# An LSTM step with one half's gates in pairs: half-width blocks, input products 128 steps at a time, and another order of VectorE's queue

## The chip, the cores and the metric

One core of one Trainium2 chip. The metric is the device time of one execution in microseconds; runs are given as the median of several.

## The reference

Two layers over x of shape 2 x 1024 x 256 (N = 2 sequences, T = 1024 steps, D = 256 features), all in float32. The first layer is an LSTM over time, added to its input:

```python
def step(carry, xw_t):
    prev_h, prev_c = carry
    a = xw_t + prev_h @ Wh                 # xw_t = x[:, t] @ Wx + b;  Wx, Wh: 256 x 1024
    i = sigmoid(a[:, :H]);  f = sigmoid(a[:, H:2*H])
    o = sigmoid(a[:, 2*H:3*H]);  g = tanh(a[:, 3*H:])
    next_c = f * prev_c + i * g
    next_h = o * tanh(next_c)
    return (next_h, next_c), next_h
x = x + LSTM(x, h0=cond, Wx, Wh, b)
```

The second layer is a mixture of experts over all 2048 tokens, added to its input: two shared experts (silu(x w1) * (x w3) w2, 512 hidden units each), a router over the token and the condition with sigmoid scores, the two best of eight routed experts (gelu, 256 hidden units each), their outputs weighted by normalised scores, all divided by 4.

## The kernel before

The LSTM is a chain of 1,024 dependent steps and sets the order of everything; the experts' work is put between the steps as filler.

**One step.** The hidden state is kept transposed: 128 partitions, K = 2 halves of features, and the N = 2 columns of one step. As stationary operand a step takes 32 columns (`h_at(t)`), of which only the two of this step are not zero. The recurrent weights stream as moving operand, so that ps[m] (PSUM, one tile for each half m of the units) holds, for each of Q = 4 row groups of 32 rows, the 32 rows of TB = 16 steps x 2 sequences and 4 gates x 32 units as columns. The four matmuls of a block (q = 0..3) go to four row groups. `BLOCKS` gives the order (L541): feature half k, unit half m, columns c0 to c1. k = 0 needs the first h of the step before, k = 1 the second.

After that, for m = 0, 1: VectorE transposes ps[m] in blocks of 32 x 32 (`transpose`, L568), so that units are partitions; ScalarE takes the sigmoid of three gates and the tanh of the fourth for the two rows of this step (`squash`, L571, L572); VectorE multiplies the old cell by the forget gate (`forget`, L575), copies g (`seen`, L579) and makes the new cell by a scan (L580); ScalarE takes its tanh (L588); VectorE multiplies by the output gate and writes h (`output`, L591). All instructions of an engine run in the order in which they are written.

**Input products.** ps[m] of the next 16 steps is begun ahead with bias and x Wx (`project`, L469): in 3 of 16 steps 8 matmuls (bias, then each half of x) take the place of one filler matmul.

**Filler.** In each step up to ROOM = 2 expert matmuls follow the recurrent ones (`fill.run_pe`); where there are none, matmuls on the identity (L556) keep PE busy. Their results are taken up by ScalarE (`fill.act`) and VectorE (`fill.dve`) behind the step's own instructions, by written-down costs: VectorE gets items up to 0.5 us a step. Expert work is queued by groups of 128 steps (64 at the end), each with a number of steps (`PACES`) over which it is spread: `scores` (L236), `shared_up` and `routed_up` (L321), `shared_down` (L377, L383), `routed_down` (L401), `add_expert` (L412); the router's choice is some 28 small VectorE operations (`choose`), queued like the rest or, behind the last step, in `aside`. The last 64 steps' tokens are worked on after the last step.

**Residual.** Every 16 steps POOL adds h to x into x2T (`residual`, L485), which the experts read; `met` (L625) is a VectorE copy of one column that waits for it.

**Loads.** wx on ScalarE's queue; bias, the first 32 steps of x, cond, wh, the rest of x, then all expert weights on SP's queue, at once at the start.

Of the kernel before, what the change touches and what calls it, by code (L numbers as in the profile page):

```python
# [9 lines left out]
F32 = mybir.dt.float32  # L10
# [6 lines left out]
P = 128  # L17
N = 2
# [5 lines left out]
TB = ROWS // N  # L24
E = 8
# [12 lines left out]
ROOM = 2  # L38
WARM = 5
# [5 lines left out]
BLOCKS = [(0, 0, 0, 128), (0, 1, 0, 64), (1, 0, 0, 128), (0, 1, 64, 128), (1, 1, 0, 128)]  # L45


class Fill:
# [19 lines left out]
    def to_dve(self, cost, fn, lag=1):  # L68
        self.add(self.dve, cost, fn, lag)

    def to_aside(self, cost, fn):
        if self.last:
            self.aside.append(fn)
        else:
            self.to_dve(cost, fn)

    def run_aside(self, count):
        for _ in range(min(count, len(self.aside))):
            self.aside.popleft()()
# [21 lines left out]
def lstm_moe_kernel(  # L101
# [23 lines left out]
    xT_sb = const.tile([P, K, T, N], F32, name="xT_sb")  # L125

    b_sb = const.tile([P, 4 * D], F32, name="b_sb")
    one_sb = const.tile([P, ROWS], F32, name="one_sb")
    nc.vector.memset(b_sb, 0.0)
    nc.vector.memset(one_sb, 0.0)  # L130
    nc.vector.memset(one_sb[0:1, :], 1.0)
    xT_v = xT.rearrange("(k p) t n -> p k t n", p=P)
    FIRST = 2 * TB
    nc.sync.dma_start(out=b_sb[0:1, :], in_=b)
    for k in range(K):
        nc.scalar.dma_start(out=wx_sb[:, k, :], in_=wx[k * P : (k + 1) * P, :])
        nc.sync.dma_start(out=xT_sb[:, k, :FIRST, :], in_=xT_v[:, k, :FIRST, :])
# [3 lines left out]
    for q in range(4):  # L141
        for k in range(K):
            cols = slice(max(FIRST, q * T // 4), (q + 1) * T // 4)
            nc.sync.dma_start(out=xT_sb[:, k, cols, :], in_=xT_v[:, k, cols, :])
# [8 lines left out]
    nc.sync.dma_start(out=wr_sb, in_=wrT.rearrange("(k p) e -> p k e", p=P))  # L153
    nc.sync.dma_start(out=rb_sb, in_=rbias.to_broadcast([P, E]))
    nc.sync.dma_start(out=w1_sb, in_=s_w1T.rearrange("(k p) f -> p k f", p=P))
    nc.sync.dma_start(out=w3_sb, in_=s_w3T.rearrange("(k p) f -> p k f", p=P))
    nc.sync.dma_start(out=w2_sb, in_=s_w2T.rearrange("(c p) d -> p c d", p=P))
    nc.sync.dma_start(out=r1_sb, in_=r_w1T.rearrange("(k p) f -> p k f", p=P))
    nc.sync.dma_start(out=r2_sb, in_=r_w2T.rearrange("(c p) d -> p c d", p=P))
# [21 lines left out]
    stepp = ctx.enter_context(tc.tile_pool(name="step", bufs=3))  # L181
    stepsp = ctx.enter_context(tc.tile_pool(name="steps", bufs=2))
# [34 lines left out]
    def experts(t0, S):  # L217
# [42 lines left out]
        def squash():  # L260
            st["s"] = big("s")
            nc.scalar.activation(st["s"], st["z"], AF.Sigmoid)
            for fn in choose():
                fill.to_aside(0.18, fn)
# [131 lines left out]
        def routed_down(i, e2, j):  # L396
            if j == 0:
                st["down"] = bank()
            ps, half, h = st["down"], j // (HR // P), j % (HR // P)
            c = (2 * e2 + half) * (HR // P) + h  # L400
            nc.tensor.matmul(  # L401
                ps[:, half, :], toks(st["h_r"][:, c, :], i), r2_sb[:, c, :],
                start=(h == 0), stop=(h == HR // P - 1), skip_group_check=True,
            )
            if j == 2 * (HR // P) - 1:
                for half in range(2):
                    fill.to_dve(0.5, lambda half=half: add_expert(i, 2 * e2 + half, ps[:, half, :]))

        def add_expert(i, e, ps):
            fill.run_aside(len(fill.aside))  # L410
            acc = st["acc", i]
            nc.vector.scalar_tensor_tensor(  # L412
                acc, ps, st["gate"][:, i, e : e + 1], acc, ALU.mult, ALU.add
            )
            if e % 2:
                fill.let_go()
            if e == E - 1:
                t = t0 + i * (P // N)
                nc.sync.dma_start(out=out_tn[t : t + P // N], in_=acc)
# [27 lines left out]
    SLOT = K * ROWS  # L447
    DIAG = SLOT + N
    hs, diags = [], []
    for i in range(2):  # L450
        flat = const.tile([P, TB * DIAG], F32, name=f"h{i}")
        nc.gpsimd.memset(flat, 0.0)
        hs.append(flat[:, : TB * SLOT].rearrange("p (u k r) -> p u k r", k=K, r=ROWS))
        diags.append(flat.rearrange("p (u s) -> p u s", s=DIAG)[:, :, :SLOT])

    def h_at(t):
        return hs[t // TB % 2][:, t % TB]

    def h_cols(t):
        u = t % TB  # L460
        return h_at(t)[:, :, N * u : N * (u + 1)]
# [3 lines left out]
    def project(ps, grp, k):  # L465
        for m in range(K):
            for q in range(Q):
                cols = slice(q * D + m * P, q * D + (m + 1) * P)
                nc.tensor.matmul(  # L469
                    ps[m][q * ROWS : (q + 1) * ROWS],  # L470
                    one_sb if k < 0 else xT_sb[:, k, grp * TB : (grp + 1) * TB, :],
                    b_sb[:, cols] if k < 0 else wx_sb[:, k, cols],
                    start=(k < 0),
                    stop=False,
                    skip_group_check=True,
                )

    def gates_tile():

        tiles = [gates_ps.tile([P, 4, P], F32, name=f"ps{m}") for m in range(K)]  # L480
        return [a[:, 0] for a in tiles], [a[:, 1] for a in tiles], tiles[0][:, 2:]

    def residual(grp, u0, u1):
        t0 = grp * TB - 1
        nc.gpsimd.tensor_add(  # L485
            x2T[:, :, t0 + u0 : t0 + u1, :],
            xT_sb[:, :, t0 + u0 : t0 + u1, :],
            diags[grp % 2][:, u0:u1].rearrange("p u (k r) -> p k u r", r=ROWS)[:, :, :, :N],
        )
# [23 lines left out]

    nxt_results = results()
# [5 lines left out]
    nxt, nxt_turned, busy = gates_tile()  # L520
# [5 lines left out]
    for k in range(-1, K):  # L526
        project(nxt, 0, k)
    due = 0
    for t in range(T):
        fill.step = t  # L530
        grp, u = divmod(t, TB)
        if u == 0:
            ps, turned = nxt, nxt_turned
            nxt, nxt_turned, busy = gates_tile()
            fresh = True
            sgm, gf = nxt_results


        for k, m, c0, c1 in BLOCKS:
            for q in range(Q):  # L540
                nc.tensor.matmul(  # L541
                    ps[m][q * ROWS : (q + 1) * ROWS][:, c0:c1],
                    h_at(t)[:, k, :],
                    wh_sb[:, k, q * D + m * P + c0 : q * D + m * P + c1],
                    start=False,
                    stop=(u == TB - 1 and k == K - 1),
                    skip_group_check=True,
                )
        ahead = t + TB < T and u in (1, 6, 11)
        if ahead:  # L550
            project(nxt, grp + 1, u // 5 - 1)
            fresh = False
# [8 lines left out]
        rows = slice(N * u, N * (u + 1))  # L561

        gT = [turned[m].rearrange("p (a r) -> p a r", r=ROWS) for m in range(K)]
# [6 lines left out]
        def squash(m):  # L570
            nc.scalar.activation(sgm[:, u, m, :, :, 1], gT[m][:, 0:3, rows], AF.Sigmoid)  # L571
            nc.scalar.activation(gf[:, u, m, :, 0], gT[m][:, 3, rows], AF.Tanh)  # L572

        def forget(m):
            nc.vector.tensor_mul(gf[:, u, m, :, 1], sgm[:, u, m, 1, :, 1], c_prev[m][:, :, 1])  # L575
# [14 lines left out]
        def output(m):  # L590
            nc.vector.tensor_mul(h_cols(t + 1)[:, m], sgm[:, u, m, 2, :, 1], cells[m][:, 2, :, 0])  # L591
# [15 lines left out]
        if u == TB - 1:  # L607
            residual(grp, int(grp == 0 or t - TB in ends), TB)
        if t == 2 * TB:
            lg = bank()[:, 0, :E]  # L610
            fill.banks -= 1
            fill.pe.extend((0, lambda k=k: condition_scores(lg, k)) for k in range(K))
        if t in ends:
            residual(grp + 1, 0, 1)
            if t == T - 1:
                drain(fill)
                fill.last = True
                fill.banks += 4
            t0, S, pace = ends[t]
            experts(t0, S)  # L620
            due = t + pace
        if u == TB // 2 and t > TB:

            met = stepp.tile([P, 1], F32, name="met")
            nc.vector.tensor_copy(met, x2T[:, 0, t - u - 2, :1])  # L625
        fill.run(fill.dve, 0.5)
# [3 lines left out]
def drain(fill):  # L630

    while fill.pe or fill.act or fill.dve:
        fill.step += 1
        fill.run_pe(4)
        fill.run(fill.act, 100.0)
        fill.run(fill.dve, 100.0)
        fill.run_aside(3)
# [65 lines left out]
```

## Time and profile before

| | |
|---|---|
| median of 3 runs | 2315.3 us (2314.7 to 2316.05) |
| the profiled execution | 2314.89 us, its span 2313.1 us |
| TensorE clock granted | 1.00 |
| PE busy (records) | 2220.1 us, 96% (48,816) |
| VectorE busy | 1701.6 us, 74% |
| ScalarE busy | 885.3 us, 38% |
| POOL busy | 25.9 us, 1% |
| chain that ended last | VectorE 59%, PE 37%, issue 3% |
| L541, passes of 128 and of 64 columns | 277 and 219 ns, 24,576 and 16,384 |
| L568, transposes of 128x128 | 332 ns, 2,048 |

How to read it: the busy table counts records; PE's are pipelined and their ends modelled, so that passes of four row groups overlap in it. The chain is followed back from the last instruction, at each step to what released it. Lines such as "L568 DVE STREAM_TRANSPOSE ps<-ps 128x128" are one group: line of the kernel, engine, operation, output and input tile, and shape; the number behind "idle before" is the time for which the engine stood still just before these instructions, with what ended it.

### The profile page before, as it was taken

The page shows a single profiled execution, that of the slowest core. Times are in us where ns is not written, and L with a number is a line of the kernel's source. Part 1 is how long each engine was busy: PE and PEld are TensorE (multiplying, and loading weights), DVE is VectorE, ACT ScalarE, POOL GpSimd, SP SyncE. Part 2 cuts the span into 40 slices and gives each one's busy share as a digit, 9 for nine tenths or more (in the row PEclk, how much of TensorE's full clock was granted, in tenths as well). Part 3 has the DMA queues.
Part 4 walks back from the last instruction along what each step waited for, and adds up shares of the span by engine and source line. Part 5 has one row for each costly group of instructions (what it writes and reads, how often), then busy time and mean ns, then how long its engine had stood idle before and what let it go on. Part 6 is the DMA issues. An engine that isn't in the chain of part 4 may idle for free.

```text
span 2313.1 us, 115407 instructions
## 1 busy us (share of the span) xinstructions
PE 2220.1 (96%) x48816; PEld 1574.3 (68%) x48816; DVE 1701.6 (74%) x10961; ACT 885.3 (38%) x6427; POOL 25.9 (1%) x82
## 2 busy tenths in 40 slices
PE   9999999999999999999999999999999999999978
PEld 6666666666666666666666666666666666666657
DVE  5666677777777777777777777777777777777775
ACT  3333334433334333443334333343333433344342
POOL 0000000000000000000000000000000000000000
PEclk9999999999999999999999999999999999999999
DMA  5000000000000000000000000000000000000000
GB/s 203 3 3 3 3 3 3 3 6 5 3 3 4 5 6 3 3 3 6 6 3 3 3 6 5 3 3 3 5 6 3 3 3 5 6 3 3 8 4 7
DMA packets 9705, 21.03 MB, mean 9 GB/s; under 512 B 1761, under 2 KB 7137, under 8 KB 8930
## 3 DMA queue, kind: packets, MB, share of 16 engines
q1 hardware_dynamic: 8898, 12.61, 1.6%
q8 instruction: 381, 6.24, 1.1%
q14 instruction: 138, 1.13, 0.2%
q10 hardware_dynamic: 288, 1.05, 0.1%
HBM read 11.56 MB, written 2.10 MB: 6 GB/s over the span
## 4 chain that ended last, share of the span: by engine, by line
DVE 59%; PE 37%; issue 3%; DMA 0%; SPq 0%; ACT 0%
PE ps L541 35%; DVE ps L568 29%; DVE c L580 12%; DVE results L575 8%; DVE seen L579 7%; DVE h L591 3%; PE ps L321 0%; PE ps_f L401 0%; PE ps_f L321 0%; PE ps L401 0%; DMA wh_sb<-in_wh_dram 0%; PE ps_f L383 0%; PE ps L383 0%; PE ps L556 0%; DVE acc L412 0%
## 5 line engine op out<-in xcount | busy, mean ns | idle before, releaser
L541 PE MATMUL ps<-wh_sb,h 128*32 128x128 f32 (+1 forms) x40960 | 1112.7, 254 | 86.9 <-DVE h L591 22.9
L541 PEld LDWEIGHTS ps<-wh_sb,h 128*32 128x32 f32 x40960 | 837.3, 109 | 489.9 <-DVE h L591 488.0
L568 DVE STREAM_TRANSPOSE ps<-ps 128x128 f32<-128x128 f32 x2048 | 677.8, 332 | 416.4 <-PE ps L541 415.0
L571 ACT ACTIVATE results<-ps 128x6 f32<-128x6 f32 x2048 | 362.9, 177 | 1167.3 <-DVE ps L568 1071.5
L556 PE MATMUL ps<-ident 128*128 128x256 f32 x1954 | 575.4, 391 | 0.0
L591 DVE TENSOR_TENSOR h<-results,c 128x2 f32<-128x2 f32 x2048 | 314.2, 153 | 168.2 <-ACT c L588 168.1
L556 PEld LDWEIGHTS ps<-ident 128*128 128x128 f32 x1954 | 351.4, 189 | 83.3 <-issue 45.1
L588 ACT ACTIVATE c<-c 128x2 f32<-128x2 f32 x2048 | 321.5, 157 | 220.1 <-DVE c L580 180.6
L580 DVE TENSOR_TENSOR_SCAN c<-results 128x4 f32<-128x4 f32 x2048 | 359.0, 175 | 0.0
L572 ACT ACTIVATE results<-ps 128x2 f32<-128x2 f32 x2048 | 340.4, 166 | 0.0
L579 DVE COPY seen<-results 128x2 f32<-128x2 f32 x2048 | 330.9, 162 | 0.0
L575 DVE TENSOR_TENSOR results<-results,c 128x2 f32<-128x2 f32 x2048 | 320.7, 157 | 0.0
L321 PE MATMUL ps_f<-x2T,r_sb 128*128 128x256 f32 (+1 forms) x800 | 166.8, 360 | 0.0
L321 PE MATMUL ps_f<-x2T,w_sb 128*128 128x256 f32 (+1 forms) x800 | 166.6, 360 | 0.0
L401 PE MATMUL ps_f<-r_sb,h_r 128*128 128x256 f32 x488 | 162.0, 424 | 0.0
L321 PEld LDWEIGHTS ps_f<-x2T,r_sb 128*128 128x128 f32 (+1 forms) x800 | 77.8, 153 | 42.7 <-issue 42.0
L321 PEld LDWEIGHTS ps_f<-x2T,w_sb 128*128 128x128 f32 (+1 forms) x800 | 77.6, 153 | 42.5 <-issue 41.8
L401 PEld LDWEIGHTS ps_f<-r_sb,h_r 128*128 128x128 f32 x488 | 75.4, 188 | 43.4 <-issue 40.5
L383 PE MATMUL ps_f<-w_sb,h_s 128*128 128x256 f32 x240 | 80.1, 425 | 0.0
L469 PE MATMUL ps<-wx_sb,xT_sb 128*32 128x128 f32 x2048 | 79.4, 273 | 0.0
L412 DVE SCALAR_TENSOR_TENSOR acc<-ps_f,gate,acc 128x256 f32<-128x256 f32 x122 | 58.2, 477 | 4.4 <-PE ps_f L401 4.2
L469 PEld LDWEIGHTS ps<-wx_sb,xT_sb 128*32 128x32 f32 x2048 | 58.6, 110 | 0.0
(81 smaller groups left out, 473.5 us busy)
## 6 DMA issues: line engine op xcount, KB each, us to landing
r_sb<-in_r_w1T_dram SPq DMA_DIRECT2D x1, 2048.0 KB, 17.2
r_sb<-in_r_w2T_dram SPq DMA_DIRECT2D x1, 2048.0 KB, 18.5
out_dram<-acc SPq DMA_DIRECT2D x16, 128.0 KB, 2.1
xT_sb<-in_xT_dram SPq DMA_DIRECT2D x6, 256.0 KB, 6.5
wx_sb<-in_wx_dram ACTq DMA_DIRECT2D x2, 512.0 KB, 4.2
wh_sb<-in_wh_dram SPq DMA_DIRECT2D x2, 512.0 KB, 4.4
w_sb<-in_s_w1T_dram SPq DMA_DIRECT2D x1, 1024.0 KB, 7.6
w_sb<-in_s_w3T_dram SPq DMA_DIRECT2D x1, 1024.0 KB, 9.6
```

What stands on the lines that cost most here:

```text
L321: nc.tensor.matmul(ps[r : r + rows, half, :W], w[:, k, c * P + r : c * P + r + rows], mov[k], start=(k == 0), stop=(k == K - 1), skip_grou ...
L401: nc.tensor.matmul(ps[:, half, :], toks(st["h_r"][:, c, :], i), r2_sb[:, c, :], start=(h == 0), stop=(h == HR // P - 1), skip_group_check= ...
L541: nc.tensor.matmul(ps[m][q * ROWS : (q + 1) * ROWS][:, c0:c1], h_at(t)[:, k, :], wh_sb[:, k, q * D + m * P + c0 : q * D + m * P + c1], sta ...
L556: nc.tensor.matmul(busy, ident, ident.unsqueeze(1).to_broadcast([P, 2, P]), start=fresh, stop=False, skip_group_check=True,)
L568: nc.vector.transpose(turned[m], ps[m])
L571: nc.scalar.activation(sgm[:, u, m, :, :, 1], gT[m][:, 0:3, rows], AF.Sigmoid)
L572: nc.scalar.activation(gf[:, u, m, :, 0], gT[m][:, 3, rows], AF.Tanh)
L575: nc.vector.tensor_mul(gf[:, u, m, :, 1], sgm[:, u, m, 1, :, 1], c_prev[m][:, :, 1])
L579: nc.vector.tensor_copy(seen[m], gf[:, u, m, :, 0])
L580: nc.vector.tensor_tensor_scan(c_new[m].rearrange("p n z -> p (n z)"), sgm[:, u, m, 0].rearrange("p n z -> p (n z)"), gf[:, u, m].rearrang ...
L588: nc.scalar.activation(cells[m][:, 2, :, 0], c_new[m][:, :, 1], AF.Tanh)
L591: nc.vector.tensor_mul(h_cols(t + 1)[:, m], sgm[:, u, m, 2, :, 1], cells[m][:, 2, :, 0])
```

## The change

Half 1's gates are kept in two pairs. ps[1] has 64 columns (two gates x 32 units) in place of 128; the first pair lies in rows 0 to 15 of each row group and the second in rows 16 to 31, so one tile lasts TH = 8 steps and not 16. The stationary operand becomes a window over h (`h_window`) that places the two columns at the right row, with zeros around. BLOCKS has 7 entries and 28 matmuls a step in place of 5 and 20: half 1's blocks are 64 or 32 columns wide, with the same 512 columns in all. The second transpose is 128x64.

Input products are made for 128 steps at once (`queue_inputs`, `input_product`) as filler with wx as stationary operand, evacuated by ScalarE with the bias added (`keep_inputs`), and put into ps[m] by a matmul on the identity (`inject`), every 8 steps for half 1 and every 16 for half 0; in these steps one filler matmul is left out. Block 0's first 16 steps are made before the loop.

The residual moves from POOL to VectorE, and `met` goes. VectorE's filler queue takes the router's operations from `aside` (cost 0.18, several in one step if the budget allows), holds back `add_expert` (late=True) until `aside` is empty, and is not run in the last step of each 16. Loads are reordered: the first 16 steps of x, bias, cond, wh, x to step 128; everything else is issued from step 4 on. A sigmoid before the loop loads ScalarE's table.

```diff
-BLOCKS = [(0, 0, 0, 128), (0, 1, 0, 64), (1, 0, 0, 128), (0, 1, 64, 128), (1, 1, 0, 128)]
+BLOCKS = [
+    (0, 0, 0, 0, 128),
+    (0, 1, 0, 0, 32),
+    (1, 0, 0, 0, 128),
+    (0, 1, 0, 32, 64),
+    (0, 1, 1, 0, 64),
+    (1, 1, 0, 0, 64),
+    (1, 1, 1, 0, 64),
+]
...
+    def run_dve(self, budget):
+        while True:
+            ready, cost, fn, late = self.dve[0] if self.dve else (0, 0.0, None, True)
+            if fn and ready <= self.step and cost <= budget and not (late and self.aside):
+                self.dve.popleft()
+            elif self.aside and budget >= ASIDE:
+                cost, fn = ASIDE, self.aside.popleft()
+            else:
+                return
+            budget -= cost
+            fn()
...
+    def h_window(t, k, m, pair):
+        at = EDGE + t % TB * ROWS - N * (t % TH if m else t % TB) - pair * PAIR
+        return hs[t // TB % 2][:, k, at : at + ROWS]
...
+    def inject(ps, m, grp):
...
+        for q in range(Q):
+            if m == 0:
+                x_rows, cols = blocks[blk][:, q, at : at + ROWS], ident
+            else:
+                x_rows = block_half1(blk)[:, q // 2, at // PAIR].rearrange("p c r -> p (c r)")
+                cols = ident[:, q % 2 * 64 : q % 2 * 64 + 64]
+            nc.tensor.matmul(
+                ps[q * ROWS : (q + 1) * ROWS], x_rows, cols,
+                start=True, stop=False, skip_group_check=True,
+            )
...
     def residual(grp, u0, u1):
-        nc.gpsimd.tensor_add(
+        nc.vector.tensor_add(
...
+        if t == 4:
+            load_rest()
+            queue_inputs(0, ROWS)
+            queue_inputs(1)
...
-        for k, m, c0, c1 in BLOCKS:
+        for k, m, pair, c0, c1 in BLOCKS:
             for q in range(Q):
+                w0 = q * D + m * P + pair * 64
                 nc.tensor.matmul(
-                    ps[m][q * ROWS : (q + 1) * ROWS][:, c0:c1],
-                    h_at(t)[:, k, :],
-                    wh_sb[:, k, q * D + m * P + c0 : q * D + m * P + c1],
+                    ps[m][q * ROWS : (q + 1) * ROWS, c0:c1],
+                    h_window(t, k, m, pair),
+                    wh_sb[:, k, w0 + c0 : w0 + c1],
...
-        ahead = t + TB < T and u in (1, 6, 11)
+        ahead = t + 1 < T and t % TH == TH - 1
         if ahead:
-            project(nxt, grp + 1, u // 5 - 1)
-            fresh = False
+            for m, steps in ((0, TB), (1, TH)):
+                if (t + 1) % steps == 0:
+                    inject(nxt[m][0], m, (t + 1) // steps)
...
+        if u < TB - 1:
+            fill.run_dve(0.5)
+            continue
+        residual(grp, int(grp == 0 or t - TB in ends), TB)
```

## The prediction

> **What bounds the kernel now.** I read the page first: engines, then the chain.
>
> ```profile
> PE 2220.1 (96%) x48816; PEld 1574.3 (68%) x48816; DVE 1701.6 (74%) x10961; ACT 885.3 (38%) x6427; POOL 25.9 (1%) x82
> ...
> DVE 59%; PE 37%; issue 3%; DMA 0%; SPq 0%; ACT 0%
> ```
>
> PE's 96% is not the limit: the chain runs mostly on VectorE, and no engine fills it. It is a loop of 1,024 dependent steps. The chain around 1,203 us shows its links (start, length):
>
> ```profile
> 1203.66 0.80 PE ps L541 x24
> ...
> 1204.49 0.66 DVE ps L568 x2
> ```
>
> One step is h (L591), the recurrent matmuls (L541), two transposes (L568), gates on ScalarE (L571, L572), the cell (L575 to L580), h. VectorE's timeline over the same step gives the order and the period, 1205.98 - 1203.77 = 2.21 us (2.208 in the median of all steps, from the single starts):
>
> ```profile
> 1203.77 0.16 DVE L591 TENSOR_TENSOR h<-results,c 128x2 f32<-128x2 f32 x1 [0.17 <-ACT c L588]
> 1203.85 0.42 DVE L344 TENSOR_TENSOR h_s<-ps_f,y 128x256 f32<-128x256 f32 x1
> 1204.49 0.66 DVE L568 STREAM_TRANSPOSE ps<-ps 128x128 f32<-128x128 f32 x2 [0.22 <-PE ps L541]
> 1205.06 0.16 DVE L575 TENSOR_TENSOR results<-results,c 128x2 f32<-128x2 f32 x1
> ...
> 1205.39 0.16 DVE L575 TENSOR_TENSOR results<-results,c 128x2 f32<-128x2 f32 x1
> ...
> 1205.98 0.16 DVE L591 TENSOR_TENSOR h<-results,c 128x2 f32<-128x2 f32 x1 [0.16 <-ACT c L588]
> ```
>
> ScalarE's timeline says what each half waits for:
>
> ```profile
> 1204.85 0.18 ACT L571 ACTIVATE results<-ps 128x6 f32<-128x6 f32 x1 [1.11 <-DVE ps L568]
> ...
> 1205.18 0.18 ACT L571 ACTIVATE results<-ps 128x6 f32<-128x6 f32 x1
> ```
>
> Half 0's sigmoid starts 0.03 after transpose 0 ends, half 1's 0.03 after transpose 1 ends (1204.82 + 0.33), and each half's L575 starts 0.03 after its sigmoid ends. Half 1's L575 at 1205.39 could come some 0.06 earlier for VectorE's queue (0.08 behind the scan at 1205.25). So **the end of transpose 1 sets the step**, with 0.06 us to gain before half 0's cell takes over. Transpose 1 in turn starts when half 1's last matmul is out: transpose 0 leaves VectorE free earlier, since L575 can follow a transpose by 0.24. A shorter transpose 1 pays; later half 1 matmuls cost one for one.
>
> **The recurrent matmuls.** By form:
>
> ```profile
> L541 PE MATMUL ps<-wh_sb,h 128*32 128x128 f32 x24576 | 1112.6, 277 | 86.9 <-DVE h L591 22.9 <-DMA wh_sb<-in_wh_dram 1.2 <-issue 0.9
> ...
> L541 PE MATMUL ps<-wh_sb,h 128*32 128x64 f32 x16384 | 603.8, 219 | 0.0
> ```
>
> Each matmul is two records (40 a step for 20 in the code). The four row groups q run side by side: their starts lie 7 ns apart, and the next block's pass follows 110 ns later behind 128 columns, 55 behind 64. (Medians 273 and 219: 54 ns less for 64 columns fewer.) A pass of 32 columns is not in the trace. By the slope it takes 28 ns, and its four issues 4 x 7 = 28. Its weights load beside the pass before: the first matmul of a step, with nothing before it, shows 298 at most against 273, so 25 ns of load. Three things meet at 28, so I take 28, with 55 (the 64-column row) as the upper bound. Below 28 nothing speaks for it.
>
> Half 0's second block needs h of half 1: its weight load starts 0.053 after that h ends. With 28 ns passes in the piece before it, PE is free early and the weight load decides (0.053 + 0.025); now PE's queue does, 0.009 later. Gain 0.009. From that block's end to the start of half 1's last pass there are now 2 x 55 + 110 = 220 ns, and 2 x 28 + 5 x 55 = 331 after the change: +0.111. The last pass then takes 219 instead of 273: -0.054. With the 0.009, transpose 1 starts **0.049 later** (rounded up).
>
> **Transpose 1** goes from 128 to 64 columns (332 ns now, L568). Nearest rows: VectorE's 128x256 and 128x128 products out of PSUM, 416 and 281 ns (L340), 1.05 ns a column; 64 columns are 67 ns, so 265. The upper gain is everything above the 157 ns of a 2-column operation spread over 126 columns, 1.4 ns: 243. The lower is none: 332. I take 265, as L340 reads PSUM too. End of transpose 1: +0.049 - 0.067 = -0.018. Half 0 starts 0.009 earlier and stays ahead. **1,024 x 0.018 = -18.4 us**.
>
> [...]
>
> **Other edits.**
> Input products: 1,536 matmuls at L469 go; 192 products (128 steps at once) and 768 identity matmuls come. The former stood in place of one filler matmul in 3 of 16 steps; the new ones do the same or fill L556's place. PE has room: in the single starts the last filler pass is modelled to end 0.06 us before the next step's first weight load, and at other changes of tile form that load starts 0.07 before such an end. So 0.13 are free, of which 0.049 + 0.018 go. Cost 0; if the cover were gone, up to 0.07 in a step. ScalarE gets 64 evacuations of 128x256, 381 ns each by L338, at most two a step in its 1.11 us gap: 0; uncovered 24 us.
>
> L485's adds move from POOL to VectorE: some 64 of about 64 columns, 0.22 us each between the 167 ns of 16 columns and 281 of 128; they stand behind the last h of a 16-step group, where the timeline has 0.64 us until the transpose and no other filler runs. 0; uncovered 14 us. In 18 steps the POOL add stood beside a scan, which took 0.26 instead of 0.17 (363.46), and the step was 0.09 longer: **-1.6 us**.
>
> VectorE's queue order. Now PE still owes work when the last step ends:
>
> ```profile
> 2272.05 3.32 PEld L383 LDWEIGHTS ps_f<-w_sb,h_s 128*128 128x128 f32 x16 [0.20 <-issue]
> ...
> 2282.30 0.63 PEld L236 LDWEIGHTS ps<-wr_sb,x2T 128*128 128x128 f32 x4
> ```
>
> The last 64 steps' scores (L236) wait behind 24 matmuls of the tokens before (L383, L401), though h was done at 2273.5. In the changed build's order nothing of those is left behind the last step: only two fillers, then the scores. They can start when the two VectorE adds (0.22 + 0.15) are through, near 2273.9: **-8.4 us**. The 28 matmuls behind keep their order.
>
> Start. First transpose at 9.82, held by wh (1.33 us of wait). wh's DMAs are issued about 1.3 us earlier behind fewer bytes, but the first gates now need 64 small products over two PSUM buffers, ScalarE's copies and the identity matmuls, which end near 8.5: warming matmuls to 5.9, four rounds of products (8 passes of 28 ns each) and copies (near 0.2 each, by L511's 225 ns for 32 columns) with two in flight, then 0.33 for the identity matmuls; half a step follows. **-0.5** (-1.3 to +1).
>
> Loading phase. One step now waits while 9 MB of weights arrive:
>
> ```profile
> 26.66 1.08 PE L541 MATMUL ps<-wh_sb,h 128*32 128x128 f32 x39
> 28.60 0.27 PE L541 MATMUL ps<-wh_sb,h 128*32 128x128 f32 x1 [0.85 <-issue]
> ```
>
> The 40th record comes 0.85 late for nothing but issue. The page's instruction queue moved 381 packets, 6.24 MB, for 97,632 PE records: 256 instructions a packet. Under load a packet's cycle was about 6.2 us; PE uses one in 256 / 88 steps = 6.4 us now and in 256 / 120 = 2.13 steps = 4.67 us after. Some four packets fall in the load, each up to 1.5 late: 6 in place of the 1.4 lost now (two steps of 3.30 and 2.48 us instead of 2.21), rounded to **+4** (0 to +8).
>
> **Sum.** -18.4 - 1.6 - 8.4 - 0.5 + 4 = -24.9. The profiled execution took 2314.89 (span 2313.1), 0.4 under the median of 2315.3; 2314.9 - 24.9 = **2290**.
>
> **Rivals.**
> (1) Slower: 32-column passes cost as much as 64-column ones. Behind the second block the stream is then 440, and transpose 1 starts 0.111 later and ends 0.044 later; half 1 follows. 1,024 x 0.044 = +45; with the rest, -6.5: 2353. It decides from 40 ns a pass on. For it: no row of 32, and the load must fit too. Against: the 7 ns spacing and the 25 ns load. [...] 0.12. A transpose that stays at 332 would end in nearly the same place (+0.049: 2358); 0.04.
> (2) Transpose 1 at 243: ends 0.040 earlier, 2268. For it: a transpose takes 51 ns more than L340 at the same size, perhaps by block of 32. 0.10.
> (3) Passes of about 35 ns: the loop gains 4 ns only, 2304. 0.12.
> (4) Passes near 40: the loop gives the end's gain back, about 2315. 0.05.
> (5) Instruction supply binds all along: every 0.1 us over 4.67 a packet costs 1,024 / 2.13 x 0.1 = 48 us, about 2340 and more. Against: at 2140 to 2270 the steps carry nearly as many instructions now, and L541's weight loads waited for h alone. 0.04.
> (6) The order at the end doesn't save what it says (fillers late elsewhere): 2298, within my case.
> My case, 2278 to 2301: 0.53.
>
> **How the numbers follow.** Faster by over 0.2% (4.6 us, about what a measurement of this kernel can tell from no change): 0.53 + 0.10 + 0.12 = 0.75; same 0.05; slower 0.12 + 0.04 + 0.04 = 0.20. Range: 2264 (below case 2) to 2325 (beyond cases 3 and 4); rivals 1 and 5 are left out. My case alone: 2278 to 2301.
>
> **What would show it.** Right: transposes in two forms, 332 and near 265; 32-column rows about 190 ns (219 - 28); steps of 2.19 us; scores within 0.6 us of the last h; few issue waits past 60 us. Wrong: transpose 1 waiting for PE over 0.10 longer than now (rival 1), a step at 2.17 (rival 2), issue waits before L541's successor throughout (rival 5), idle VectorE time before the transposes that a filler fills.

## The result, and the profile after

The changed kernel takes 2302.0 us (median of five runs, 2300.7 to 2303.15) against 2315.0 for the kernel before on the same chip: a ratio of 0.9944, interval 0.993 to 0.9958. Forecast was 2290. The profiled execution has a span of 2300.8 us against 2313.1, so 12.3 us went where the prediction expected 24.9.

Between the first h and the last the loop lost 4.9 us, the stretch behind the last h shrank from 39.75 to 30.62 us (-9.1), and the first h came 1.75 us later (11.32 before, 13.07 after). The loop's 4.9 are, to within 0.3, three terms: 1,023 steps at 2.200 in place of 2.208 us (medians of the single starts; -8.2), the 18 long steps beside a POOL add that are gone (-1.5), and long steps while the weights arrive (+5.1).

**The forms.** From the groups of instructions by form: busy us and mean ns of one behind the first bar, idle time before them behind the second.

```profile
L638 PE MATMUL ps<-wh_sb,h 128*32 128x64 f32 x24576 | 535.2, 220 | 4.4 <-issue 4.4
L638 PE MATMUL ps<-wh_sb,h 128*32 128x32 f32 x16384 | 501.0, 194 | 0.0
...
L669 DVE STREAM_TRANSPOSE ps<-ps 128x128 f32<-128x128 f32 x1024 | 339.1, 331 | 396.9 <-PE ps L638 396.7
L669 DVE STREAM_TRANSPOSE ps<-ps 128x64 f32<-128x64 f32 x1024 | 272.1, 266 | 74.1 <-PE ps L638 6.1
```

The new transpose takes 266 ns (forecast 265). A 32-column record is 26 ns shorter than a 64-column one; by the starts, the pass behind a 32-column pass follows 28 ns later, as forecast. The last line's idle time is new: between the two transposes VectorE now stands still for 74.1 us in all, 72 ns a step. The profile names what ended it for 6.1 us only. The single starts say that it is half 1's matmuls: transpose 1 starts 0.306 us behind the start of the last pass here, and 0.307 in e1, e2 and e5.

**One step**, VectorE's timeline:

```profile
1203.19 0.16 DVE L692 TENSOR_TENSOR h<-results,c 128x2 f32<-128x2 f32 x1 [0.16 <-ACT c L689]
...
1203.89 0.66 DVE L669 STREAM_TRANSPOSE ps<-ps 128x128 f32<-128x128 f32 x2 [0.21 <-PE ps L638]
1204.46 0.16 DVE L676 TENSOR_TENSOR results<-results,c 128x2 f32<-128x2 f32 x1
...
1204.80 0.16 DVE L676 TENSOR_TENSOR results<-results,c 128x2 f32<-128x2 f32 x1
...
1205.39 0.16 DVE L692 TENSOR_TENSOR h<-results,c 128x2 f32<-128x2 f32 x1 [0.17 <-ACT c L689]
```

The two transposes still fill 0.66 us between them, though the second is 66 ns shorter: it starts 58 ns later (medians: 1.102 us behind the h before, 1.044 in the kernel before) and ends 8 ns earlier.

**The loading phase**, TensorE's timeline:

```profile
32.28 0.54 PE L638 MATMUL ps<-wh_sb,h 128*32 128x64 f32 x24 [0.89 <-issue]
...
38.47 0.43 PE L638 MATMUL ps<-wh_sb,h 128*32 128x64 f32 x16 [1.49 <-issue]
...
45.23 0.32 PE L638 MATMUL ps<-wh_sb,h 128*32 128x64 f32 x8 [2.04 <-issue]
```

Each time TensorE stops in the middle of a step's recurrent matmuls, and waits for nothing but issue. The three stops make 4.4 of the 6.5 us that long steps lose here. Behind the third the granted clock was 0.50 from 46.2 to 49.6 us, and the step that ran in it, 0.96 us too long, has no stop at all. The page's instruction queue grew with the number of instructions:

```profile
q8 instruction: 499, 8.18, 1.5%
```

Between 18 and 49 us, beside the loads, its transfers start 5.8 to 6.8 us apart; later they start 4.5 us apart in the median. TensorE uses them up at that rate: 499 transfers stand for its 127,744 records (matmuls and weight loads), 256 each, and a step of 2.200 us has 125 of them. A transfer took 0.93 to 1.16 us beside the loads and 1.08 in the median later: it is not slower there, it starts late.

**The end**, TensorE's timeline of matmuls:

```profile
2268.95 1.13 PE L655 MATMUL ps<-ident 128*128 128x256 f32 x4
2270.70 0.58 PE L255 MATMUL ps<-wr_sb,x2T 128*128 128x8 f32 x4 [0.61 <-DVE x2T L561]
```

The scores (L255) start 0.5 us after the last h (2270.19), right behind VectorE's two adds; before, they stood behind 24 matmuls, 9.2 us after h (2282.52 against 2273.35).

**A line that misleads.** The chain that ended last is now

```profile
PE 92%; DVE 7%; issue 1%; DMA 0%; SPq 0%; ACT 0%; DVEq 0%
```

where it was VectorE 59% and PE 37%. It does not say that TensorE became the bound. TensorE's filler now runs up to the next step's matmuls, so the chain, which goes back to the instruction before on the engine where it sees no wait, stays on TensorE. A kernel below (e9) takes filler out, TensorE falls to 91% busy, and its undisturbed step keeps its length.

### The profile page after: what moved, and what is told of

Same layout as the page of the kernel before. It is cut to its first block, busy times and chain, and to the rows that moved or that the text cites. A ratio compares the mean times of both kernels' runs of the same rounds, so it can differ in the third digit from the quotient of the medians.

```text
span 2300.8 us, 145499 instructions
## 1 busy us (share of the span) xinstructions
PE 2241.3 (97%) x63872; PEld 1702.9 (74%) x63872; DVE 1639.1 (71%) x10969; ACT 910.3 (40%) x6499; POOL 2.7 (0%) x9
## 3 DMA queue, kind: packets, MB, share of 16 engines
q8 instruction: 499, 8.18, 1.5%
## 4 chain that ended last, share of the span: by engine, by line
PE 92%; DVE 7%; issue 1%; DMA 0%; SPq 0%; ACT 0%; DVEq 0%
PE ps L638 51%; PE ps L655 17%; PE ps_f L339 11%; PE ps_f L419 6%; PE ps_f L401 3%; PE ps_f L507 3%; DVE ps L669 2%; DVE c L681 2%; DVE results L676 1%; DVE seen L680 1%; DVE h L692 1%; PE ps L339 0%; PE ps_f L395 0%; PE ps_f L255 0%; PE ps L419 0%
## 5 line engine op out<-in xcount | busy, mean ns | idle before, releaser
L638 PEld LDWEIGHTS ps<-wh_sb,h 128*32 128x32 f32 x57344 | 1008.3, 110 | 451.8 <-DVE h L692 446.9
L638 PE MATMUL ps<-wh_sb,h 128*32 128x128 f32 (+2 forms) x57344 | 1174.3, 231 | 51.6 <-DVE h L692 40.6
L669 DVE STREAM_TRANSPOSE ps<-ps 128x128 f32<-128x128 f32 (+1 forms) x2048 | 611.2, 298 | 471.0 <-PE ps L638 402.8
L655 PE MATMUL ps<-ident 128*128 128x256 f32 x1778 | 525.9, 387 | 0.0
L655 PEld LDWEIGHTS ps<-ident 128*128 128x128 f32 x1778 | 325.6, 190 | 49.8 <-issue 0.2
L507 PE MATMUL ps_f<-xT_sb,wx_sb 128*128 128x256 f32 (+2 forms) x384 | 79.2, 344 | 1.6 <-ACT inputs L500 1.2
L548 PE MATMUL ps<-ident,inputs 128*32 128x64 f32 (+1 forms) x1536 | 52.4, 238 | 0.1
```

Of the source, the lines that this page charges most:

```text
L638: nc.tensor.matmul(ps[m][q * ROWS : (q + 1) * ROWS, c0:c1], h_window(t, k, m, pair), wh_sb[:, k, w0 + c0 : w0 + c1], start=False, stop=(t ...
L655: nc.tensor.matmul(busy, ident, ident.unsqueeze(1).to_broadcast([P, 2, P]), start=fresh, stop=False, skip_group_check=True,)
L669: nc.vector.transpose(turned[m], ps[m])
```

## Experiments

Every time is compared with the kernel before on the same chip, which took 2312.0 to 2315.0 us there. "Lost" is the time of long steps (over 20 ns above the median) beyond that median, in the profiled execution.

**e1: no 32-column passes.** Six blocks, 24 matmuls a step.

```diff
-    (0, 1, 0, 0, 32),
+    (0, 1, 0, 0, 64),
     (1, 0, 0, 0, 128),
-    (0, 1, 0, 32, 64),
     (0, 1, 1, 0, 64),
```

> The changed kernel with the two 32-column pieces joined to one 64-column block ahead of half 0's second block (24 matmuls a step in place of 28, the same 512 columns). Theory A (the end of half 1's transpose alone sets the step): that transpose starts 0.054 us earlier, the step is 2.146 to 2.15 us and the time about 2247 us. Theory B (two coupled chains: half 0's transpose, cell and first h are as late as half 1's): half 0's transpose starts about 0.05 later relative to the last h, half 1's about 0.01 earlier, the step stays at 2.193 to 2.200 and the time at 2295 to 2303 us. Theory C (32-column passes are the loss): step gains just their extra 8 to 12 ns, 2290 to 2294 us.

2296.8 us, ratio 0.9924 (0.991 to 0.9939); step 2.197.

```profile
L668 DVE STREAM_TRANSPOSE ps<-ps 128x128 f32<-128x128 f32 x1024 | 339.3, 331 | 459.0 <-PE ps L637 458.3
L668 DVE STREAM_TRANSPOSE ps<-ps 128x64 f32<-128x64 f32 x1024 | 272.1, 266 | 6.2 <-PE ps L637 3.0
```

Transpose 0 starts 61 ns later (0.765 against 0.704 us behind half 1's h), and transpose 1 follows it at once: 6.2 us of idle time where the changed kernel has 74.1. Transpose 1 starts at 1.099 against 1.102, and the step is 3 ns shorter. The starts of the passes say why so little changes. In the changed kernel the matmuls that don't need half 1's h are through 0.299 us behind a step's first pass, TensorE waits for that h (and its weight load) until 0.344, and the last pass starts at 0.906. Here the passes run back to back and the last starts at 0.852: TensorE never waits for half 1's h. But the first pass itself, which waits for half 0's h, starts 50 ns later against half 1's h, because that h is late with transpose 0 (it starts 270 ns ahead of half 1's in place of 315). So the step is two coupled chains, one through each half: half 1's sets the changed kernel's step, half 0's sets this one's, and the two steps are 3 ns apart. The narrow passes aren't needed.

**e2: half 1's transpose over all 128 columns** (the upper 64 hold a second copy of the input products, put in by four more matmuls every 8 steps, and are not used).

```diff
-            nc.vector.transpose(turned[m], ps[m])
+            nc.vector.transpose(cur[m][4], cur[m][3])
```

> The changed kernel with half 1's transpose taken over all 128 columns again (the right 64 hold a copy of the input rows and are not used; the matmuls of the loop are as in the changed kernel, every 8 steps four more identity matmuls fill the copy). Theories A and B: the transpose takes 332 instead of 266 ns, all of it on the path, step 2.200 + 0.06 to 0.066, time 2363 to 2370 us. Rival (the shorter transpose is not on the path, the step gained elsewhere): 2302 us as before.

2370.9 us, ratio 1.0243 (1.0226 to 1.026). Transpose 1 starts where it did (1.103) and takes 331 ns; the step is 2.267. Its 65 ns come back as 67 a step: the end of transpose 1 lies on the path, one for one.

**e3: no pairs**, with all other parts of the change: `BLOCKS` of the kernel before (five blocks, 20 matmuls), both transposes over 128 columns, half 1's input products put in every 16 steps as half 0's.

> The changed kernel without the pairs: half 1 in 128 columns and 16 steps like half 0, with the five blocks of the kernel before; input products, residual, VectorE's queue and loads as changed. If the pairs are worth the 8 ns a step seen between the two traces: step 2.208, time 2308 to 2312 us. If the rest of the change, not the pairs, moved the step: 2302 us. If the pairs lose something outside the loop (instruction loading at the start: 88 instead of 120 PE instructions a step): 3 to 5 us less than by the first, 2305 to 2308 us.

2304.8 us, ratio 0.9958 (0.9944 to 0.9973). The step is back at 2.208, but only one step is long (lost: 0.75 us in the first 60 us). Against the changed kernel's 0.9944 the intervals overlap: what pairs save in the loop (8.2 us) they mostly lose in the loading phase (5.7) and, in the profiled executions, at the start (1.1, of which the pairs are not the cause: see the start below).

**e4: VectorE's queue as before** (router operations queued with the rest, `late` without effect, no budget behind the last step).

```diff
-            elif self.aside and budget >= ASIDE:
-                cost, fn = ASIDE, self.aside.popleft()
...
+            for fn in choose():
+                fill.to_aside(0.18, fn)
...
-        fill.run_dve(1.2)
+        fill.run_dve(100.0)
+        fill.run_aside(3)
```

> The changed kernel with VectorE's filler queue as before the change (the router's operations queued with the rest, no late add_expert; not run in the last step of 16, as changed). If the order of this queue is what empties PE's filler before the last step: 24 matmuls stand behind the last step again, the stretch from the last h to the end is 39 to 40 us instead of 30.6, time about 2311 us. If something else did it (steadier fill by the other edits): 2302 us.

2310.6 us, ratio 0.9982 (0.9972 to 0.9991); step 2.200, stretch behind the last h 39.16 us against 30.62. TensorE's weight loads show the old order again:

```profile
2268.13 3.32 PEld L403 LDWEIGHTS ps_f<-w_sb,h_s 128*128 128x128 f32 x16
2271.47 6.88 PEld L421 LDWEIGHTS ps_f<-r_sb,h_r 128*128 128x128 f32 x32
2278.38 0.63 PEld L256 LDWEIGHTS ps<-wr_sb,x2T 128*128 128x128 f32 x4
```

The scores (L256) stand behind 24 matmuls (48 records). The order of the queue is worth 8.5 us at the end, and in the loop nothing.

**e5: both halves in pairs.** Eight blocks of 64 columns, 32 matmuls a step.

```diff
+PAIRED = (1, 1)
...
-    (0, 0, 0, 0, 128),
-    (0, 1, 0, 0, 32),
-    (1, 0, 0, 0, 128),
-    (0, 1, 0, 32, 64),
+    (0, 0, 0, 0, 64),
+    (0, 0, 1, 0, 64),
+    (0, 1, 0, 0, 64),
+    (1, 0, 0, 0, 64),
+    (1, 0, 1, 0, 64),
     (0, 1, 1, 0, 64),
```

> The changed kernel with half 0's gates in pairs too: eight blocks of 64 columns, two for each feature half and unit half (32 matmuls a step, no 32-column pass), in the order half 0 then half 1 for the first feature half, then the same for the second; both transposes read 128x64; half 0's input products are put in every 8 steps as well. Theory B (the step is two coupled chains, one through each half's transpose, and shortening only one of them stops paying when the other is as late): both chains get shorter, the first transpose takes 266 ns instead of 332, and the step falls from 2.200 to about 2.16 us: 2301 - 1024 x 0.040 = about 2260 us. Theory A (the end of half 1's transpose alone sets the step): its matmuls end no earlier than with seven blocks, so the gain is no more than the 66 ns by which transpose 0 leaves VectorE earlier for transpose 1 only where they touch; in the changed kernel transpose 1 starts some 60 ns after transpose 0 ends, so nothing: step 2.20, 2300. Rival: instruction supply, 32 instead of 28 matmuls a step, takes part of the gain back in the loading phase: 5 us or more over the 5.1 that the changed kernel already loses there, 2265 to 2270.

2279.1 us, ratio 0.9844 (0.983 to 0.9859). The step is 2.154, 46 ns less than the changed kernel's: the passes run back to back as in e1 (the last starts at 0.862), and the shorter transpose 0 is over 70 ns before transpose 1 starts (0.723 + 0.266 against 1.059 us behind h). But 67 steps are long and lose 32.3 us in all, 13.4 of it in the first 60 us. The rival was about right for the loading phase (6.9 us over the changed kernel); the 19 us lost behind it stood in no case. The order of the blocks is not the one that the expectation describes: one of half 1's two blocks on the first h stands behind half 0's blocks on the second h.

**e6: paced loads.** The loads behind step 4 in pieces of at most 256 KB, one a step.

```diff
+            nc.vector.memset(tile_, 0.0)
+            nc.sync.dma_start(out=src[0], in_=src[1])
+        pieces.append(load)
...
-            load_rest()
+            queue_rest()
...
+        if load:
+            load()
```

> The changed kernel with the loads after step 4 cut into pieces of at most 256 KB, one issued per step from step 4 on (some 60 steps instead of 4), each held back by a one-element write of VectorE to the place it goes to. If the long steps of the loading phase are PE waiting for instructions that share the DMA engines with the weights, a quarter of their share of the engines is used at any time and the six long steps (6.5 us together) go or shrink to a few tenths each: about 2296. If instruction supply is short in itself (more instructions a step than its queue can bring), the long steps stay: 2301, or more for the added VectorE writes.

2295.4 us, ratio 0.9915 (0.99 to 0.993). No step of 1,023 is over 20 ns long. Busy time in the same stretch, first the changed kernel, then this one (TensorE, weight loads, VectorE, ScalarE, POOL, then granted clock, DMA share, GB/s):

```profile
26.00:50.00 24.00, 18.68 (x487) 14.23 (x486) 11.62 (x83) 8.96 (x58) 0.00 (x0) 0.93 0.96 348
```

```profile
26.00:50.00 24.00, 22.93 (x680) 17.88 (x680) 15.63 (x121) 12.44 (x77) 0.00 (x0) 1.00 0.31 103
```

With the DMA engines 96% busy TensorE ran 487 matmul records in these 24 us, with 31% it ran 680. The instructions themselves are the same in number; what came too seldom beside the unbroken loads were the starts of their transfers, here 3.9 to 5.3 us apart from 14 to 60 us.

**e7: the tile of zeros first.** VectorE clears `zero` ahead of its copies of cond.

```diff
+    zero = const.tile([P, TB, K, N], F32, name="zero")
+    nc.vector.memset(zero, 0.0)
     nc.vector.tensor_copy(h_cols(0), cond_sb)
...
-    zero = const.tile([P, TB, K, N], F32, name="zero")
-    nc.vector.memset(zero, 0.0)
```

> The changed kernel with one instruction moved: VectorE's clearing of the tile of zeros goes ahead of the two copies of cond, which wait for cond's transfer until 6.9 us. If ScalarE's copies of the first input products stand behind it (they come behind ScalarE's copies from the zeros), TensorE's idle stretch of 1.2 us at 7.0 to 8.2 us goes, and with it the granted clock of 0.50 to 0.67 in the slices behind: the first h comes 1 to 2 us earlier than 13.07, and the time is about 2300. If the first input products were held by something else (wx, x), first h stays at 13.07 and the time at 2302.

2300.7 us, ratio 0.9937 (0.992 to 0.9953): its interval overlaps with the changed kernel's, so by time alone the edit can't be told from nothing. The profile shows the mechanism. In the changed kernel ScalarE waits 4.45 us for `zero` (its timeline, the first line) and TensorE 1.25 us for ScalarE's copies (the second); in this kernel TensorE's wait is 0.29 (the third):

```profile
7.38 0.20 ACT L593 ACTIVATE seen<-zero 128x2 f32<-128x2 f32 x1 [4.45 <-DVE zero L582]
```

```profile
8.23 0.98 PE L507 MATMUL ps_f<-xT_sb,wx_sb 128*32 128x32 f32 x64 [1.25 <-ACT inputs L500]
```

```profile
7.39 0.82 PE L507 MATMUL ps_f<-xT_sb,wx_sb 128*32 128x32 f32 x64 [0.29 <-ACT inputs L500]
```

The first h comes at 11.75 in place of 13.07. Most of this is not the edit's: e4 has the changed kernel's order and waits 0.93 us, and its first h comes at 11.95.

**e8: e5, e6 and e7 together.**

> The three edits above together: both halves in pairs, loads after step 4 in pieces of 256 KB one per step, and the clearing of the zeros ahead of the copies of cond. If the three act in different places (the loop, the loading phase, the start), their gains add: 2302 - 41 - 6 - 1.5 = about 2253. If what pairs of half 0 gain in the loop is lost to instruction supply even without a load beside it, about 2260 or more.

2268.7 us, ratio 0.9802 (0.9788 to 0.9817): the fastest kernel of the study, but 16 us over the expected sum, which took e5's gain by its step alone. The three gains as measured (22.9, 6.7 and 1.3 us) would give 2271. The step is 2.155 and the first h at 11.61, yet 65 steps still lose 24.8 us, 20.5 of it past 160 us, where all loads are in (the last by 106). TensorE's timeline of one:

```profile
777.85 0.98 PE L657 MATMUL ps<-wh_sb,h 128*32 128x64 f32 x55 [0.20 <-DVE h L711]
779.08 0.36 PE L657 MATMUL ps<-wh_sb,h 128*32 128x64 f32 x9 [0.25 <-issue]
```

Count all records of TensorE in order of start, its waits on semaphores too, and measure a gap from one record's start to the next. Up to 2,120 us eleven gaps are 0.66 us or longer (up to 1.48); ten of them end at one place, record 193 of a block of 256, and 2.2 to 2.9 us after the start of the last 16 KB transfer of instructions. So do the gaps over 1 us, measured likewise, in the loading phases of the kernel before (2.33 us after the transfer's start), the changed kernel (2.27, 2.59, 2.59), e1 and e5. One such transfer stands for 256 records (499 for 127,744 in the changed kernel).

**e9: the input products' identity matmuls spread.** Two in each of the last four steps of eight, in place of eight in the last; a filler matmul is left out in each of the four. The edit is to e8.

```diff
-        ahead = t + 1 < T and t % min(LASTS) == min(LASTS) - 1
+        spread = t >= TB
+        ahead = t // TH * TH + TH < T and t % TH >= (TH // 2 if spread else TH - 1)
...
+            for n in [t % TH - TH // 2] if spread else range(Q):
+                m, part = divmod(n, 2)
+                inject(nxt[m][0], m, t // TH + 1, range(2 * part, 2 * part + 2))
```

> The kernel with both halves in pairs, paced loads and the earlier zeros, with the eight identity matmuls that put in the input products spread from step 16 on: two in each of the last four steps of every eight in place of all eight in the last (one filler matmul is left out in each of these four steps in place of one). In the kernel without this edit 66 steps are long, by 24.8 us together; most are step 0 or 1 of eight, and TensorE stands still for `issue` each time at the same place in its instructions, record 193 of every 256, 2.3 to 2.9 us after the last transfer of instructions began. If the supply of instructions falls short only where a burst of them (128 records of recurrent matmuls and 32 of these) meets a transfer, most of the long steps go and 10 to 20 us come back: 2250 to 2259. If 32 matmuls a step are in themselves more than the supply can bring, the lost time stays near 25 us and moves to other steps: about 2267. If the long steps are the wait for the products themselves (ScalarE's copies of them), it grows, since they are needed up to three steps earlier: above 2270.

2271.7 us, ratio 0.9827 (0.9811 to 0.9843): no gain. The long steps lose 13.5 in place of 24.8 us, but the stretch behind the last h grows from 30.3 to 37.2. That the long steps sit where bursts of instructions are is supported, not settled: the kernel also has fewer filler matmuls. It shows the misleading chain for what it is: PE 76%, and

```profile
PE 2073.2 (91%) x71860; PEld 1553.8 (69%) x71860; DVE 1570.6 (69%) x11006; ACT 910.3 (40%) x6499; POOL 2.7 (0%) x9
```

with an undisturbed step of 2.154, e8's.

**e10: e9, with filler left out only in the last of eight steps.**

```diff
             fresh = False
+            ahead = t % TH == TH - 1
```

> The kernel with the spread identity matmuls, but with a filler matmul left out only in the last of every eight steps, as in the changed kernel, not in the last four. Spreading took the lost time of long steps from 24.8 to 13.8 us, but the stretch behind the last h grew from 30.3 to 37.2 us. If that is because three filler matmuls fewer in eight steps leave expert work over, the stretch falls back to 30.3 and, with the long steps at 14 us, the time is 2262 to 2265. If the fewer long steps came from the fewer instructions (12 records in 1,130 of eight steps) and not from spreading, they are back at 25 us and the time at 2270 or above.

2280.9 us, ratio 0.9856 (0.9841 to 0.9871). The stretch behind the last h is back at 30.2, so that part of the expectation held. The other failed for a reason that none of its cases had: 395 steps are long, most of them the three in eight that follow two more matmuls and no less filler, each by 32 to 47 ns (transpose 0 starts at 0.757 to 0.771 in place of 0.723). TensorE has no room for the two matmuls and full filler in a step of this length. Whether spreading alone removes the supply's stops stays open.

**e11: e1 with paced loads and the early zeros.**

> Half 1 alone in pairs, with the six blocks that have no 32-column pass (24 matmuls a step), loads after step 4 in pieces of 256 KB one per step, and the zeros cleared ahead of the copies of cond. Without the last two edits it took 2296.84 and lost 5.0 us in four long steps; its first h came at 11.86 already. If the loads' share of the DMA engines is what makes the long steps, pacing gives those 5.0 us and the other edit next to nothing: 2291 to 2292. If the two edits gain only together with 28 matmuls a step, nothing: 2296.8.

2292.9 us, ratio 0.9904 (0.9887 to 0.992). One step is long, by 0.07 us, where e1's four lose 4.6, and the first h comes at 11.94 (e1: 11.86). Pacing gave back 4 us of time; the other edit nothing that can be seen.

## Why the prediction was right or wrong

**Right: the direction and, but for the start, each term's sign.** Transpose 266 ns (265 forecast), so neither the rival at 243 nor a transpose that stays at 332; e2 shows what the latter costs, 68.9 us over the changed kernel. 32-column passes take 28 ns (32 behind the last of a step) and 64-column ones 56, so rival 1 is not borne out. The end saved 9.1 us (8.4 forecast), and e4 gives it back when the queue's order is undone, so rival 6 falls. The POOL adds' 1.5 us (1.6 forecast) are gone: POOL is busy 2.7 us in place of 25.9, and all six long steps left lie in the loading phase. The loading phase lost 5.1 us more than before (4 forecast), mostly for the reason given: three stops make 4.4 of its 6.5 us, with transfers of instructions 5.8 to 6.8 us apart (6.2 in the prediction). Another 0.96 is the step at half the granted clock, which the prediction didn't have.

**Mis-sized: the loop, -8.2 for -18.4.** The failing term is "transpose 1 starts 0.049 later": it measured 0.058. The stretch from half 0's second block to the last pass was worked out as 331 ns and takes 343. By the starts of the passes, 8 ns lie behind the two 32-column passes: the next pass follows after 32 ns in place of 28, and the one behind it after 59 in place of 55. The other 4 are four passes at 56 in place of 55. The pass that follows after 32 starts 30 ns after its weight load, which starts with the pass before it, so it seems to wait for that load; the prediction had seen the load, 25 ns against a pass of 28, and put it at nothing. Here 9 ns against 18 are half the gain: a difference of two terms of 50 to 70 ns is only as good as the single nanoseconds in them, times 1,024. The time came out just above the prediction's own case (2278 to 2301), near rival 3's 2304, but not by that rival's wider passes. Inside the range it lies because the range was wide: the loop and the start both came out worse than forecast, and hardly anything made up for them.

The prediction also read the step too simply. It had transpose 1's end set the step, with half 0's cell 0.06 us behind it. e2 bears out the first. e1 uses up the second: half 0's transpose starts 61 ns later, and then half 0's chain sets the step, so that a last pass 54 ns earlier brings 3. With both chains shortened (e5) the step falls by 54 ns from the kernel before, 46 of them from half 0.

**Wrong sign: the start, +1.75 for -0.5.** Three things add up.

First, wh. The prediction let it come earlier because its DMAs are issued earlier. They are, by 1.1 us, but the second lands at 9.60 us (9.72 in e7) in place of 9.29. e7 shows the start with nothing else in the way; its TensorE line stands behind that of the kernel before:

```profile
9.33 0.76 PE L541 MATMUL ps<-wh_sb,h 128*32 128x128 f32 x24 [1.17 <-DMA wh_sb<-in_wh_dram]
```

```profile
9.77 0.82 PE L638 MATMUL ps<-wh_sb,h 128*32 128x128 f32 x40 [0.36 <-DMA wh_sb<-in_wh_dram]
```

It still waits for wh, and its first h, at 11.75, is 0.43 us later than before.

Second, "copies (near 0.2 each, by L511's 225 ns for 32 columns) with two in flight". The copies were as short as forecast, 0.20 each (0.80 for four), but the first could not start before 7.73, behind ScalarE's copies from `zero`, which VectorE clears behind cond's arrival at 6.9. A cost on ScalarE had been counted, its place in ScalarE's queue had not. It costs some 0.2 us, by one execution each: e4, with this order, has its first h at 11.95, e7, without it, at 11.75.

Third, the clock. In the changed kernel's profiled execution TensorE stood still for 1.25 us, and behind it the granted clock was 0.50 from 8.69 to 12.10 us. Its windows, granted clock third from the end, and then the same windows of e4, which waits 0.93 us:

```profile
9.00:10.00 1.00, 1.00 (x34) 0.70 (x29) 0.00 (x0) 0.70 (x4) 0.00 (x0) 0.50 0.53 169
10.00:11.00 1.00, 1.00 (x36) 1.00 (x35) 0.00 (x0) 0.00 (x0) 0.00 (x0) 0.50 0.00 0
```

```profile
9.00:10.00 1.00, 0.95 (x34) 0.57 (x29) 0.00 (x0) 0.53 (x3) 0.00 (x0) 1.00 0.48 160
10.00:11.00 1.00, 1.00 (x54) 0.91 (x46) 0.48 (x2) 0.18 (x2) 0.00 (x0) 1.00 0.00 0
```

The kernel before shows 1.00 there too. With this order the first h comes at 11.86 to 12.37 where the clock stays up (e1, e2, e3, e4) and at 12.93 to 13.12 where it falls (the changed kernel, e5, e6). So about 1.1 of the 1.75 us are the clock of this execution (an estimate: 13.07 less e4's 11.95), and the 1.3 us that e7's first h comes earlier are mostly the same.

**Instruction supply, rival 5, was nearly the right worry.** Put at 0.04 as a bound "all along", it does not bind in the changed kernel outside the loading phase. It binds there as the number of instructions grows, with the same loads in the first four kernels (stops are TensorE's idle times over 0.3 us that end with issue):

| matmuls a step | kernel | lost in the first 60 us | of it in stops |
|---|---|---|---|
| 20 | e3 | 0.75 us | 0.5 us |
| 24 | e1 | 4.6 us | 3.9 us |
| 28 | changed | 6.5 us | 4.4 us |
| 32 | e5 | 13.4 us | 8.6 us |
| 28, paced loads | e6 | 0 | 0 |

Part of the difference is steps at half the granted clock, which follow the longest stops in the changed kernel and in e5, and not in e1 and e3: from 28 to 60 us the granted clock was 0.95 and 0.84 in the first two on average, and 1.00 in the others. In the other kernels with 28 matmuls and unbroken loads (e2, e4, e7) the stops make 3.8 to 4.7 us, so by the stops alone 24 and 28 can't be told apart.

At 32 it also binds without a load: in e8 a transfer of instructions starts every 4.0 us in the median, 4.53 in the changed kernel (4.67 was forecast).

## What to carry to other kernels

Where a step is two coupled chains, shorten both or expect a fraction of the gain: pairs in half 1 gave 8 ns a step, pairs in both 54. Split matmuls cost instructions: 8.18 MB of them were moved here for 6.24 before, in transfers that started 5.8 to 6.8 us apart beside loads that kept the DMA engines 96% busy, and 3.9 to 5.3 us apart with paced loads (31%). Issue the loads in pieces over the steps in which they aren't needed yet, and count instructions per microsecond before splitting further. A load that is issued earlier need not land earlier (wh: issued 1.1 us earlier, landed 0.3 later): look at its landing. When an operation moves to another engine, look up what stands ahead of it in that engine's queue (here copies that waited 4.45 us), not only how long it takes (0.20).

## What the runs showed of the hardware that was not expected

- TensorE's stops for instructions ended at one place. In the kernel before one gap of 1.13 us and in the changed kernel three, of 1.09, 1.71 and 2.26 us, all in the loading phase, end at record 193 of a block of 256, 2.3 to 2.6 us after the start of the last 16 KB transfer of instructions; in e8 ten of the eleven longest do, at 2.2 to 2.9 us. The longest idle time of a recurrent matmul that ended with issue was 0.9 us in the kernel before (20 matmuls a step), 2.0 in the changed kernel (28) and 3.1 in e5 (32).
- In the changed kernel the granted clock was 0.50 twice between the first matmul and the last, for 3.41 us each: from 8.69 to 12.10 us and from 46.23 to 49.65. In the 3.41 us ahead of these TensorE was busy for 1.77 and 1.37 us; with 1.85 us of the 3.41 from 35.99, the clock stayed at 1.00 in the next. So TensorE had been busy for half of the time or a little less before the clock fell. One idle stretch alone did not tell: at the start the clock fell to 0.50 behind stretches of 0.40 and 1.25 us in the changed kernel, 0.69 and 0.95 in e5, 0.74 and 1.42 in e6, and stayed at 1.00 behind 0.57 and 0.93 in e4, 0.50 and 1.04 in e3, and 1.43 alone in e2. What decides is not shown.
